# Sixteen groups of attention heads: the first groups' side work dealt out anew, and the loads, clip and norm of two late groups moved

## The chip, the cores and the metric

The kernel runs on one core of a Trainium2 chip. A core has a matrix engine (TensorE, PE in the profile), a vector engine (VectorE, DVE), a scalar engine (ScalarE, ACT), a general engine (GpSimd, POOL) and SyncE (SP), which here only issues transfers. Each engine works through its own list of instructions in order, and waits on semaphores for the others. The metric is the device time of one execution in microseconds; the kernel before takes 945.73 us, the median of three runs (945.61 to 947.5).

## The reference: what is computed

Eight sequences of 512 tokens with 256 channels pass through two layers. Only what matters is shown:

```python
# layer 0
xn = layernorm(x)
x = x + attention(xn) + int8_linear(xn)
# attention: 16 heads of 64, rotary turn of q and k, causal softmax, times v, times Wo, + bo
x_scale = max(|xn|.max() / 127, 1e-5)          # one number for all sequences
x_int8 = clip(round(xn / x_scale), -128, 127)
int8_linear = (x_int8 @ weight_int8.T) * x_scale * weight_scale + bias
# layer 1
xn = layernorm(x)
comparison = (xn @ left) @ (xn @ right).T / 16
x = x + (comparison > threshold) * softmax(comparison + gate_bias) @ xn
      + sigmoid(xr @ W_r) * (relu(xk @ W_k)**2 @ W_v)   # xr, xk mix a token with the one before
```

Since x_scale needs all eight sequences, the int8 part of layer 0 can only begin once all inputs were normed.

## The kernel before, in words

**Groups.** The attention of a sequence is cut into two groups of eight heads. Group `at` (0 to 15) belongs to sequence `at // 2`. Group 0 is written out by hand, groups 1 to 14 are passes of the loop `for at in range(1, last)`, with `last` = 15 (group 14 leaves the loop in the middle), and group 15 with the second layer follows. The text writes (at, run) or (head group, which) where the code does.

**Steps of a group.**
- `project_qk` (L403): q or k of four heads by matmul into pq; ACT moves it to l with the bias (L408); four transfers on SP's queue bring the swapped halves to y (L410).
- `turn_own` multiplies l by a cosine table into h (DVE, L420); `turn_other` multiplies y by a sine table (DVE, L420) and adds it to h (POOL, L435).
- `project_v` (L445): v by matmul in two halves, moved by ACT (L451), written to DRAM; `load_v` reads it back rearranged into vr (L462). vr has one buffer, so the load waits for the matmul `weigh` of the group before.
- A group's scores are done in five runs. `scores(at, run)` is PE (L482). `soften(at, run)` adds the mask and finds the row maximum on DVE (L508), then takes the exponential on ACT with its row sum (L512). `divide(at, run)` takes the reciprocal of the sum on DVE (L523) and multiplies p on POOL (L528). `turn(at, run)` transposes p in 32 x 32 blocks on DVE (L548) into t.
- `weigh(at)` is the matmul of t with vr (av, L565), which needs all five runs turned; `keep_weighed` moves it on ACT (L579); `finish` multiplies by Wo (pw, L365) and adds to x1 (L374).

**Order.** The scheduling is manual: every engine's list follows the order of the calls in the text. In pass `at` of the loop that is scores(at, 0), the last turn of group at - 1, weigh(at - 1), the turns of q and k of later groups, then runs 1 to 4 of group `at` mixed with the projections of groups at + 1 and at + 2.

**Side work.** Input x of a sequence is loaded, its mean and variance taken (`look_at`, statistics L152 to L157: DVE, then one power on POOL), normalised and its largest value found (`prepare`, L170 and L304 on DVE), transposed on PE (`transpose_x`, pxt, L321) and moved by ACT. In the loop, look_at(b + 2) and prepare(b + 2) stand in the second group of a sequence b, from group 1 on, and transpose_x(b + 1) in the first group of sequence b. In group 1 the int8 weights and the constants of layer 1 are spread as well (`spread_rest`, `spread_second`, L285, L140, L141).

**The two groups that complete sequences.** In groups 12 and 13 (`last - 3`, `last - 2`) the int8 part is added to sequences 0 and 1. Their unfinished sums come back from DRAM as x1e (L180) and their normed input as xnl (L183). `quantise` rounds and clips xnl into xq, three instructions on POOL (L190 to L192); `add_quantised` multiplies (acc, L207) and adds. At the end of group 13 the normed first sequence of layer 1 is made (`first_norm`, yn, L170), which PE transposes in the stage after group 14 (pyt, L231). The third sequence's input, xnl_2, is fetched in group 15, and its clip stands on DVE (`clip`, L198, L199), as do those of all later ones.

**Buffers.** Eight PSUM banks go round among all matmul results. The tiles p come from a pool of four buffers, x and vr have one each, and xnl one of its own.

Of the kernel before, what the change touches and what calls it, by code (L numbers as in the profile page):

```python
# [44 lines left out]
def two_layers(  # L45
# [97 lines left out]
    def statistics(src, name, parts=1, power=True):  # L143

        st = small.tile([P, NT, 6], F32, tag="st", name=f"st_{name}", bufs=2)
        mv = small.tile([P, NT, 2], F32, tag="mv", name=f"mv_{name}", bufs=2)
        ve = small.tile([P, NT], F32, tag="ve", name=f"ve_{name}", bufs=2)
        rstd = small.tile([P, NT], F32, tag="rstd", name=f"rstd_{name}", bufs=2)
        for h in range(parts):
            rows = slice(h * NT // parts, (h + 1) * NT // parts)  # L150
            for t in range(NT)[rows]:
                nc.vector.bn_stats(st[:, t, :], src[:, t, :])  # L152
            for t in range(NT)[rows]:
                nc.vector.bn_aggr(mv[:, t, :], st[:, t, :])
            nc.vector.tensor_scalar(ve[:, rows], mv[:, rows, 1], LN_EPS, None, ALU.add)
            if power:
                nc.gpsimd.tensor_tensor(rstd[:, rows], ve[:, rows], mhalf[:, rows], ALU.pow)  # L157
        if power:
            return mv, rstd

        def later():
            nc.gpsimd.tensor_tensor(rstd, ve, mhalf, ALU.pow)
            return mv, rstd

        return later
# [20 lines left out]
    def quantise(b, r, xq):  # L186

        r = r.rearrange("p a n -> p (a n)")
        xq_ = xq.rearrange("p k n -> p (k n)")
        nc.gpsimd.tensor_scalar(r, r, xs[:, 1:2], ROUND, ALU.mult, ALU.add)  # L190
        nc.gpsimd.tensor_scalar(xq_, r, -ROUND, -128.0, ALU.add, ALU.max)
        nc.gpsimd.tensor_scalar(xq_, xq_, 127.0, 127.0, ALU.min, ALU.min)  # L192
# [64 lines left out]
    with ExitStack() as c0:  # L257
# [26 lines left out]
        def spread_rest():  # L284
            nc.vector.tensor_copy(w8b, rest.pop(0).bitcast(I8))  # L285
            nc.gpsimd.tensor_tensor(bob, bob, rw[:, 2, :], ALU.add)
# [143 lines left out]
        def turn_other(at, which):  # L430

            _, y = evicted.pop((at, which))
            h = heads_of[at, which]
            times(y, y, S)
            nc.gpsimd.tensor_tensor(h, h, y, ALU.add)  # L435

        def project_v(at):
            b, g = divmod(at, NH)
            stores[at] = away.tile([4, P, NT * P], F32, tag="v", name=f"va_{at}")
            for half in range(2):  # L440
# [48 lines left out]
        def soften(at, run):  # L489
# [7 lines left out]
            for us in RUNS[run]:  # L497
                if (at, run) == (last, 0):
                    p = qk.tile([P, 2, S], F32, tag="h0", name=f"p_{at}_{us[0]}")
                else:  # L500
                    p = prob.tile([P, 2, S], F32, tag="p", name=f"p_{at}_{us[0]}")
# [16 lines left out]
        def divide(at, run):  # L518
            _, sm, rs = sums_of[at]
            for us in RUNS[run]:  # L520
                first = 2 * PLACE[us[0]]
                which = slice(first, first + 2 * len(us))
                nc.vector.reciprocal(rs[:, which], sm[:, which])  # L523
                for i in us:
                    for e in range(2):
                        c = 2 * PLACE[i] + e
                        p = chances[at, i][:, e, :]
                        nc.gpsimd.tensor_scalar(p, p, rs[:, c : c + 1], 1.0, ALU.mult, ALU.mult)  # L528
# [74 lines left out]
        def round_late(b):  # L603
            r = late[b].rearrange("p a n -> p (a n)")
            nc.gpsimd.tensor_scalar(r, r, xs[:, 1:2], ROUND, ALU.mult, ALU.add)
# [162 lines left out]
        turn_other(1, 0)  # L768
        turn_other(1, 1)
# [16 lines left out]
        divide(0, 1)  # L786
# [3 lines left out]
        scores(0, 2)  # L790
        soften(0, 2)
        project_qk(3, 0)
        transpose_x(1)
        turn_qk(3, 1)
        turn(0, 1)
        divide(0, 2)
        scores(0, 3)
        soften(0, 3)
        project_v(1)
        turn_qk(3, 0)  # L800
        x_next.append(load_x(2))
        turn(0, 2)
        divide(0, 3)
        scores(0, 4)
        soften(0, 4)
        turn(0, 3)
        project(2, 1)
        divide(0, 4)
        for at in range(1, last):
# [20 lines left out]
            load_v(at)  # L830
            divide(at, 0)
# [16 lines left out]
            turn(at, 1)  # L848
            divide(at, 2)
            if g == 1 and b + 2 < B:  # L850
# [3 lines left out]
            if at == 1:  # L854
                spread_rest()
                spread_second()
# [19 lines left out]
            if at == last - 2:  # L876
                first_norm()
# [31 lines left out]
        late[2] = fetch_input(2, work.tile([P, NK, S], F32, tag="xnl", name="xnl_2"))  # L909
# [9 lines left out]
        load_v(at)  # L919
        add_biases(B - 1)  # L920
# [145 lines left out]
```

## Time and profile before

| what | value |
|---|---|
| runs | 945.61, 945.73, 947.5 us |
| profiled execution | 950.06 us |
| its span | 948.3 us |
| PE busy | 927.3 us, 98% of the span |
| DVE, ACT, POOL busy | 784.0, 529.7, 568.3 us |
| mean TensorE clock granted | 0.996 |

The profiled execution is 1.76 us longer than its span, and 4.33 us above the median of the runs. A view called the timeline lists instructions of one engine in order: the start in us from the span's start, the length in us, the engine, the line of the kernel, the operation, out<-in, shapes, how many alike in a row, and in brackets the idle time of the engine before the first, with what ended it. "issue" there means that the profile shows nothing that the engine waited for. The matmuls of fp32 are two records each. A row of windows shows, for a stretch of time, its length, the busy us of PE, of the weight loads (PEld), DVE, ACT and POOL with counts, then the clock granted to TensorE (1.00 is full), the busy share of the DMA engines and the GB/s. Since PE's own busy time includes slow matmuls, idle time and slow stretches are read from the timeline and the windows together.

### The profile page before, as it was taken

What the parts mean: (1) busy time and instruction counts of PE and PEld (TensorE: products, weight loads), DVE (VectorE), ACT (ScalarE), POOL (GpSimd) and SP (SyncE); (2) the same over time, 40 slices, a digit from 0 to 9 for tenths busy, and PEclk for the clock granted to TensorE, in tenths of its full rate; (3) what the DMA queues carried; (4) which work ended last, traced back from release to release, by engine and by line L of the source; (5) the groups of instructions that cost most, each with busy time, mean ns of one, the idle gap of its engine ahead of it and who ended that gap; (6) DMA issues with size and microseconds to landing.
All of it is one profiled execution on the core that took longest, in us unless ns stands there. A gap on an engine that the chain in (4) does not pass through costs nothing.

```text
span 948.3 us, 27434 instructions
## 1 busy us (share of the span) xinstructions
PE 927.3 (98%) x10491; PEld 601.3 (63%) x10491; DVE 784.0 (83%) x2425; ACT 529.7 (56%) x1480; POOL 568.3 (60%) x702
## 2 busy tenths in 40 slices
PE   9999999999999999999999998999999999999998
PEld 5446566656666575657566655666657777777776
DVE  4888988898799789878997896798989588888864
ACT  3565565656564646574656655555567334455553
POOL 3795775655664757557565665989776424444311
PEclk9999999999999999999999999999999999999999
DMA  7666454525443545263444435353344132221110
GB/s 213 187 169 170 113 129 145 123 78 134 150 107 103 127 122 135 70 177 94 110 114 134 114 90 157 113 157 90 91 123 125 46 96 66 67 66 44 32 34 33
DMA packets 60930, 105.40 MB, mean 111 GB/s; under 512 B 7552, under 2 KB 38272, under 8 KB 60800
## 3 DMA queue, kind: packets, MB, share of 16 engines
q1 hardware_dynamic: 58928, 102.01, 39.7%
q10 hardware_dynamic: 1872, 1.64, 0.6%
q8 instruction: 83, 1.36, 0.6%
q14 instruction: 47, 0.39, 0.1%
HBM read 39.14 MB, written 28.84 MB: 72 GB/s over the span
## 4 chain that ended last, share of the span: by engine, by line
PE 94%; DVE 2%; issue 2%; POOL 1%; ACT 1%; DMA 0%; DVEq 0%; POOLq 0%; ACTq 0%
PE pq L403 22%; PE av L565 14%; PE sc L482 13%; PE pw L365 12%; PE pv L445 11%; PE po L725 6%; PE pk L672 3%; PE pg L687 3%; PE pvv L699 3%; PE c L644 2%; PE trc L712 1%; PE plr L242 1%; PE acc L207 1%; PE pyt L231 1%; DVE p L508 1%
## 5 line engine op out<-in xcount | busy, mean ns | idle before, releaser
L512 ACT ACTIVATE p<-p,nm 128x64 f32<-128x64 f32 (+15 forms) x512 | 260.0, 511 | 144.8 <-DVE nm L508 111.1
L528 POOL TENSOR_SCALAR p<-p,rs 128x64 f32<-128x64 f32 (+15 forms) x512 | 269.5, 549 | 44.4 <-DVE rs L523 42.2
L435 POOL TENSOR_TENSOR h<-h,y 128x1024 f32<-128x1024 f32 x64 | 167.0, 2610 | 176.2 <-DVE y L420 97.1
L508 DVE CUSTOM_DVE_ANT_0 p<-sc,cmask 128x64 f32<-128x64 f32 (+15 forms) x512 | 190.4, 434 | 73.8 <-PE sc L482 73.8
L548 DVE STREAM_TRANSPOSE t<-p 128x256 f32<-128x256 f32 (+3 forms) x640 | 192.4, 365 | 20.2 <-POOL p L528 20.2
L482 PE MATMUL sc<-h,h 64*32 64x512 f32 (+15 forms) x4096 | 141.6, 396 | 7.0 <-issue 3.6
L565 PE MATMUL av<-t,vr 32*64 32x384 f32 (+15 forms) x4096 | 130.8, 396 | 6.7 <-issue 6.7
L565 PEld LDWEIGHTS av<-t,vr 32*64 32x64 f32 x4096 | 124.5, 132 | 12.6 <-issue 11.1
L482 PEld LDWEIGHTS sc<-h,h 64*32 64x32 f32 x4096 | 78.6, 106 | 84.1 <-issue 63.2
L408 ACT ACTIVATE l<-pq,cs 128x512 f32<-128x512 f32 x128 | 84.4, 682 | 61.7 <-PE pq L403 52.1
L420 DVE TENSOR_TENSOR y<-y,cs 128x1024 f32<-128x1024 f32 x64 | 111.1, 1736 | 5.1 <-DMA y<-l 4.5
L445 PE MATMUL pv<-wv,xnT 128*128 128x512 f32 x256 | 114.0, 598 | 1.3 <-ACT l L408 1.3
L403 PE MATMUL pq<-xnT,wq 128*128 128x512 f32 x256 | 115.0, 601 | 0.2 <-ACT xnT L324 0.2
L365 PE MATMUL pw<-wo,att 128*128 128x256 f32 x512 | 114.8, 382 | 0.0
L403 PE MATMUL pq<-xnT,wk 128*128 128x512 f32 x256 | 112.9, 593 | 0.0
L365 PEld LDWEIGHTS pw<-wo,att 128*128 128x128 f32 x512 | 95.9, 190 | 18.5 <-issue 6.1
L512 ACT ACTIVATION_READ_ACCUMULATOR p<-p,nm 128x1 f32 x512 | 96.9, 189 | 0.0
L445 PEld LDWEIGHTS pv<-wv,xnT 128*128 128x128 f32 x256 | 47.4, 190 | 59.3 <-issue 54.0
L403 PEld LDWEIGHTS pq<-xnT,wk 128*128 128x128 f32 x256 | 48.6, 190 | 55.6 <-issue 54.9
L420 DVE TENSOR_TENSOR h<-l,cs 128x1024 f32<-128x1024 f32 x64 | 79.7, 1246 | 4.3 <-ACT l L408 4.3
L403 PEld LDWEIGHTS pq<-xnT,wq 128*128 128x128 f32 x256 | 47.4, 191 | 56.4 <-issue 48.8
L579 ACT ACTIVATE att<-av,cs 128x512 f32<-128x512 f32 x64 | 38.8, 689 | 72.4 <-PE av L565 72.4
(113 smaller groups left out, 956.0 us busy)
## 6 DMA issues: line engine op xcount, KB each, us to landing
y<-l SPq DMA_DIRECT2D x256, 128.0 KB, 2.3
va<-v SPq DMA_DIRECT2D x32, 512.0 KB, 3.0
vr<-va SPq DMA_DIRECT2D x64, 256.0 KB, 4.4
x<-in_x SPq DMA_DIRECT2D x15, 512.0 KB, 5.3
xnf<-xnT SPq DMA_DIRECT2D x8, 512.0 KB, 3.3
x1f<-x SPq DMA_DIRECT2D x7, 512.0 KB, 2.6
out<-y SPq DMA_DIRECT2D x14, 256.0 KB, 2.2
cut_wo<-xnf SPq DMA_DIRECT2D x5, 512.0 KB, 4.5
```

The costliest lines, as they stand in the source:

```text
L365: nc.tensor.matmul(pw[:, j, :], atts[at, p][:, tok], wo[:, 4 * (at % NH) + p, :], start=(p == 0), stop=(p == 3),)
L403: nc.tensor.matmul(pb, w[:, g, k, bass.ts(t, P)], xnT[b][:, k, :], start=(k == 0), stop=(k == NK - 1),)
L408: nc.scalar.activation(l[:, t, :], pb, AF.Identity, bias=cs[:, bias : bias + 1])
L420: nc.vector.tensor_tensor(dst, src, table[:, None, :].to_broadcast([P, 2, S]), ALU.mult)
L435: nc.gpsimd.tensor_tensor(h, h, y, ALU.add)
L445: nc.tensor.matmul(pb.rearrange("p (g n) -> p g n", g=2), xnT[b][:, k, bass.ts(2 * half + j, P)], wqkv[2][:, 2 * g : 2 * g + 2, k, :], sta ...
L482: nc.tensor.matmul(scored[at, i][e][j * Q : j * Q + Q, :], q[rows, j % 2, bass.ts(i, Q)], k[rows, j % 2, :n], start=True, stop=True,)
L508: nc.vector.tensor_tensor_reduce(p[:, e, col : col + n], sc, cmask[:, S - n :], -1.0 / L**0.5, BIG, ALU.add, ALU.min, nm[:, c : c + 1],)
L512: nc.scalar.activation(p[:, e, col : col + n], p[:, e, col : col + n], AF.Exp, bias=nm[:, c : c + 1], scale=-1.0, accum_out=sm[:, c : c + 1],)
L528: nc.gpsimd.tensor_scalar(p, p, rs[:, c : c + 1], 1.0, ALU.mult, ALU.mult)
L548: nc.vector.transpose(turned[at][c][:, :, at_ : at_ + (n - 1) * pitch(c) + 1 : pitch(c), :], p[:, :, c * P : c * P + n * Q].rearrange("p e ...
L565: nc.tensor.matmul(banks[j][e * L : e * L + L, i * Q :], vs[at][rows, m, c, bass.ts(e, L)], t[c][rows, e, m * pitch(c) + m : m * pitch(c) ...
```

## The change

In groups 0 and 1:
- the additions of h for q and k of the second four heads of group 0 go from POOL to DVE;
- of runs 1 and 3 of group 0, the division of the last tile (p_12, p_8) goes from POOL to ACT, as Copy with a scale per row;
- q of head group 3 is projected and moved by ACT ahead of the exponentials of run 2; the reciprocals of run 2 stand ahead of the multiplication of y, and the division of run 2 ahead of POOL's addition of h;
- the second half of v of group 1 is projected after the scores of run 4, whose softmax step moves ahead of the turn of run 2, with its p in the buffer of xnl;
- one small DVE instruction (ve) of the second input moves behind the additions.

In groups 1 to 4: look_at(2) and prepare(2) move from group 1 to group 2, the spreads from group 1 to group 4.

In groups 12 and 13: x1e and xnl are fetched after load_v instead of at the start of the pass; the two clipping instructions go from POOL to DVE, behind turn(at, 1); the normalising of `first_norm` moves from the end of group 13 to group 14, behind divide(at, 1). In group 15 xnl_2 is fetched after load_v.

```diff
-            nc.vector.tensor_scalar(ve[:, rows], mv[:, rows, 1], LN_EPS, None, ALU.add)
             if power:
+                nc.vector.tensor_scalar(ve[:, rows], mv[:, rows, 1], LN_EPS, None, ALU.add)
                 nc.gpsimd.tensor_tensor(rstd[:, rows], ve[:, rows], mhalf[:, rows], ALU.pow)
...
         def later():
+            nc.vector.tensor_scalar(ve, mv[:, :, 1], LN_EPS, None, ALU.add)
...
-    def quantise(b, r, xq):
+    def round_input(r):
         r = r.rearrange("p a n -> p (a n)")
-        xq_ = xq.rearrange("p k n -> p (k n)")
         nc.gpsimd.tensor_scalar(r, r, xs[:, 1:2], ROUND, ALU.mult, ALU.add)
-        nc.gpsimd.tensor_scalar(xq_, r, -ROUND, -128.0, ALU.add, ALU.max)
-        nc.gpsimd.tensor_scalar(xq_, xq_, 127.0, 127.0, ALU.min, ALU.min)
...
-            nc.gpsimd.tensor_tensor(h, h, y, ALU.add)
+            (engine or nc.gpsimd).tensor_tensor(h, h, y, ALU.add)
...
+                elif (at, run) == (0, len(RUNS) - 1):
+                    p = work.tile([P, 2, S], F32, tag="xnl", name=f"p_{at}_{us[0]}")
...
-                        nc.gpsimd.tensor_scalar(p, p, rs[:, c : c + 1], 1.0, ALU.mult, ALU.mult)
+                        if on_act and us is RUNS[run][-1]:
+                            nc.scalar.activation(p, p, AF.Copy, scale=rs[:, c : c + 1])
+                        else:
+                            nc.gpsimd.tensor_scalar(p, p, rs[:, c : c + 1], 1.0, ALU.mult, ALU.mult)
...
-        turn_other(1, 0)
-        turn_other(1, 1)
+        turn_other(1, 0, nc.vector)
+        turn_other(1, 1, nc.vector)
...
-        divide(0, 1)
+        divide(0, 1, on_act=True)
         turn_other(2, 0)
         project_qk(3, 1)
         load_v(0)
         scores(0, 2)
+        project_qk(3, 0)
         soften(0, 2)
-        project_qk(3, 0)
         transpose_x(1)
-        turn_qk(3, 1)
+        turn_own(3, 1)
+        divide(0, 2)
+        turn_other(3, 1)
         turn(0, 1)
-        divide(0, 2)
         scores(0, 3)
+        project_v(1, (0,))
         soften(0, 3)
-        project_v(1)
-        turn_qk(3, 0)
-        x_next.append(load_x(2))
-        turn(0, 2)
-        divide(0, 3)
         scores(0, 4)
         soften(0, 4)
+        project_v(1, (1,))
+        turn_qk(3, 0)
+        divide(0, 3, on_act=True)
+        divide(0, 4)
+        turn(0, 2)
+        x_next.append(load_x(2))
         turn(0, 3)
         project(2, 1)
-        divide(0, 4)
...
-            if at in (last - 3, last - 2):
-                s_ = at - last + 3
-                fetch_output(s_, output_tile(f"x1e_{s_}"))
-                xnl = fetch_input(s_, work.tile([P, NK, S], F32, tag="xnl", name=f"xnl_{s_}"))
             scores(at, 0)
...
             load_v(at)
+            if at in (last - 3, last - 2):
+                s_ = at - last + 3
+                fetch_output(s_, output_tile(f"x1e_{s_}"))
+                xnl = fetch_input(s_, work.tile([P, NK, S], F32, tag="xnl", name=f"xnl_{s_}"))
             divide(at, 0)
...
             turn(at, 0)
-            if g == 1 and b + 2 < B:
+            if at == 2:
+                look_at(2)
+            elif at == 4:
+                spread_rest()
+                spread_second()
+            elif g == 1 and 1 <= b < B - 2:
                 look_at(b + 2)
             divide(at, 1)
+            if at == last - 1:
+                first_norm()
             project(at + 1, 0)
             if at in (last - 3, last - 2):
-                xq = work.tile([P, NK, S], BF16, tag="xq", name=f"xq_{s_}")
-                quantise(s_, xnl, xq)
+                round_input(xnl)
...
             turn(at, 1)
+            if at in (last - 3, last - 2):
+                xq = work.tile([P, NK, S], BF16, tag="xq", name=f"xq_{s_}")
+                clip(xnl, xq)
             divide(at, 2)
-            if g == 1 and b + 2 < B:
+            if at == 2:
+                prepare(2)
+            elif g == 1 and 1 <= b < B - 2:
                 prepare(b + 2)
...
             if at == 1:
-                spread_rest()
-                spread_second()
+                nc.gpsimd.tensor_tensor(bob, bob, rw[:, 2, :], ALU.add)
                 add_biases(0)
...
             finish(at - 1)
-            if at == last - 2:
-                first_norm()
...
         fetch(B - 1)
-        late[2] = fetch_input(2, work.tile([P, NK, S], F32, tag="xnl", name="xnl_2"))
...
         load_v(at)
+        late[2] = fetch_input(2, work.tile([P, NK, S], F32, tag="xnl", name="xnl_2"))
```

More of the change, by code (lines that the diff above doesn't have):

```diff
@@ L285, in spread_rest @@
             nc.vector.tensor_copy(w8b, rest.pop(0).bitcast(I8))
-            nc.gpsimd.tensor_tensor(bob, bob, rw[:, 2, :], ALU.add)
         xnT = {}
@@ L428, in turn_own, with turn_other @@
             heads_of[at, which] = h
-        def turn_other(at, which):
+        def turn_other(at, which, engine=None):
             _, y = evicted.pop((at, which))
@@ L434, in turn_other, with project_v @@
             times(y, y, S)
-            nc.gpsimd.tensor_tensor(h, h, y, ALU.add)
-        def project_v(at):
+            (engine or nc.gpsimd).tensor_tensor(h, h, y, ALU.add)
+        def project_v(at, halves=(0, 1)):
             b, g = divmod(at, NH)
-            stores[at] = away.tile([4, P, NT * P], F32, tag="v", name=f"va_{at}")
-            for half in range(2):
+            if 0 in halves:
+                stores[at] = away.tile([4, P, NT * P], F32, tag="v", name=f"va_{at}")
+            for half in halves:
                 v = work.tile([P, 4, 2, P], F32, tag="v", name=f"v_{at}_{half}", bufs=2)
@@ L516, in soften, with divide @@
                     col += n
-        def divide(at, run):
+        def divide(at, run, on_act=False):
             _, sm, rs = sums_of[at]
@@ L603, in round_late @@
         def round_late(b):
-            r = late[b].rearrange("p a n -> p (a n)")
-            nc.gpsimd.tensor_scalar(r, r, xs[:, 1:2], ROUND, ALU.mult, ALU.add)
+            round_input(late[b])
         def clip_late(b):
```

## The prediction

> **What bounds the kernel now.** I read the page first, then the chain that ended last, then TensorE's (PE's) timeline for every idle stretch, then the engine that ended each, and last the clock by windows and the DMA queues. From the page:
>
> ```profile
> span 948.3 us, 27434 instructions
> PE 927.3 (98%) x10491; PEld 601.3 (63%) x10491; DVE 784.0 (83%) x2425; ACT 529.7 (56%) x1480; POOL 568.3 (60%) x702
> PE 94%; DVE 2%; issue 2%; POOL 1%; ACT 1%; DMA 0%; DVEq 0%; POOLq 0%; ACTq 0%
> ```
>
> PE is the bound: 94% of the chain is matmul, and the change leaves the number of matmuls alone. What can move is the 6% (57 us) in which the chain is not on PE, and the slow matmuls behind such waits. An undisturbed group between 131 and 567 us takes 44.3 us, or 45.1 with the transposes of the next x. PE's timeline where groups take longer:
>
> ```profile
> 35.49 3.91 PE L482 MATMUL sc<-h,h 64*32 64x512 f32 x104 [1.50 <-POOL h L435]
> 76.31 9.69 PE L565 MATMUL av<-t,vr 32*64 32x512 f32 x256 [2.29 <-issue]
> 123.70 6.67 PE L565 MATMUL av<-t,vr 32*64 32x512 f32 x197 [1.41 <-issue]
> 149.70 1.04 PE L321 MATMUL pxt<-ident,x 128*128 128x128 f32 x8
> ...
> 584.78 3.16 PE L482 MATMUL sc<-h,h 64*32 64x448 f32 x60 [2.74 <-issue]
> 671.34 8.05 PE L565 MATMUL av<-t,vr 32*64 32x512 f32 x256 [1.67 <-issue]
> 705.68 1.93 PE L482 MATMUL sc<-h,h 64*32 64x512 f32 x40 [1.21 <-POOL h L435]
> 724.45 1.08 PE L482 MATMUL sc<-h,h 64*32 64x352 f32 x27 [0.89 <-issue]
> ```
>
> Columns: start, length, and in brackets the idle time before and its releaser. Where "issue" stands before av, VectorE (DVE) names the cause: its last two transposes of the group before end at that moment, held by GpSimd (POOL):
>
> ```profile
> 75.76 0.77 DVE L548 STREAM_TRANSPOSE t<-p 128x256 f32<-128x256 f32 x2 [1.06 <-POOL p L528]
> 123.16 0.77 DVE L548 STREAM_TRANSPOSE t<-p 128x256 f32<-128x256 f32 x2 [1.06 <-POOL p L528]
> 149.77 0.20 DVE L523 RECIPROCAL rs<-sm 128x4 f32<-128x4 f32 x2
> 670.80 0.77 DVE L548 STREAM_TRANSPOSE t<-p 128x256 f32<-128x256 f32 x2 [1.06 <-POOL p L528]
> ```
>
> The wait at 582 is another kind: DVE and POOL are not late. SP's queue issued 1 MB just before, and the DMA view shows no instruction packet (q8) from 576.5 to 582 us while q1 moved 1.56 MB, then one in 582 to 584:
>
> ```profile
> 576.58 0.51 SPq L180 DMA_DIRECT2D x1e<-x1f  x1
> 577.13 0.43 SPq L183 DMA_DIRECT2D xnl<-xnf  x1
> 581.32 2.67 SPq L462 DMA_DIRECT2D vr<-va  x4
> 582.00:584.00 2.00, 0.04 (x2) 0.00 (x0) 0.00 (x0) 1.58 (x3) 2.00 (x4) 1.00 0.92 246
> 586.00:588.00 2.00, 2.00 (x44) 0.90 (x29) 1.51 (x9) 1.02 (x3) 2.00 (x1) 0.50 0.41 82
> ```
>
> In the two windows (busy of PE, PEld, DVE, ACT, POOL; clock; DMA) PE stands still, then runs at clock 0.50. I read it as PE out of instructions, its fetch queued behind x1e and xnl.
>
> **The change part by part.** Names of groups are values of `at`.
>
> (a) Groups 0 and 1, to the first av. The two adds of h leave POOL (2.35 us each, from 29.58 to 35.44 with the wait between them) for DVE. DVE adds of two SBUF operands are not in the trace; the nearest row is DVE's L420, 1.22 us when POOL is still. So y_1_0 29.5, add 30.7, y_1_1 31.9, add 33.1: PE arrives at 32.93, its 1.50 us go, and the first softmax step starts near 34.2 instead of 36.60. POOL loses four divisions of p_12 and four of p_8; ACT gains them. ACT's Copy from SBUF with a scale per row is not in that stage; bounds are ACT's exponentials of these widths without their accumulator read (0.63, 0.36, 0.50, 0.44 us), so 1.9 us for each four, and half of that. The small edits here cost nothing: ve's 0.17 us on DVE falls before DVE's first softmax step and lets POOL start on x_1 at 33.3 instead of 35.4; run 4's p in xnl's buffer frees its softmax step from turn(0,2); the later half of pv is the same PE work behind 0.6 us of scores.
> The new wait: ACT's first division needs the reciprocal that DVE makes after turn(0,0), near 47.3, while ACT is done with its exponentials near 45.3. Behind it on ACT are l_3_1, l_3_0 (pulled ahead: 4 x 0.62) and the next exponentials (4.05): 47.3 + 1.9 + 2.4 + 4.05 = 55.7. DVE's reciprocal for run 2 now stands ahead of y_3_1 and waits for them, with 1.5 to 3 us idle. Then y_3_1 1.2, turn 2.8, softmax steps 2.8 and 0.7, h and y of (3,0) 2.4, reciprocals 0.3, turn 2.8: 68.7. POOL's last adds and divisions (2.36, then 1.9 and 0.93 from about 65.7) end at 70.9, turn 3 and 4 near 72.5. av can start near 72.8 against 76.31: gain 3.5, between 0 (the ACT wait eats it) and 5.5 (all four idle stretches of PE to there, 1.50 + 0.49 + 1.25 + 2.29). PE gets there near 70, so some 2.5 us idle stay.
>
> That wait's half clock stays too: 78 to 80 us ran at 0.50 after 2.29 us of idle, and that av took 9.69 us where others take 8.05, while 1.41 and 1.67 us of idle were followed by clock 1.00. [...]
>
> (b) Group 1 sheds look_at(2), prepare(2) and the spreads: 1.37 + 0.37 + 0.17 + 1.95 + 1.22 + 0.42 + 0.22 + 0.29 = 6.0 us of DVE. It is there that DVE falls behind (no idle time on DVE from 104.6 to 122.1 us). Its last turn comes over 3 us earlier, the wait of 1.41 goes: gain 1.4 (0 to 1.4). The spreads in group 4 are 0.9 us in DVE's idle time before its run 2 there: nothing; if it were gone, 0.9. POOL's one power (1.02 us) moves from group 1 to 2: nothing, POOL waits for DVE there.
>
> (c) Group 2 gets them. look_at (1.9 us) falls into DVE's idle 3.0 us before run 2: nothing. prepare does not: DVE finishes the reciprocals of run 2 at 149.97, as PE comes to the transposes of x_2 (149.70). Normalising takes 1.95 (the same four at 195.08 in group 3), PE's last five transposes 0.65 more: 152.6 instead of 150.74. Cost 1.8, from 0 (if DVE gains on PE) to 3.4 (idle long enough for a half clock, 1.6). ACT's copies of xnT shift along; behind them amax 1.22 delays no PE, which has run 3 in hand.
>
> (d) Group 12: x1e and xnl are issued after vr instead of before it, past one step of SP's queue, at about 584 in before's time. The fetch at 582 then finds only x1_6. Gain: run 1 of the scores took 6.77 us where others take 2.05, the next pq 7.50 instead of 7.06: 5.1. Between 0 (it stands anyway) and 5.1. [...] xnl lands near 590, POOL wants it at 595.9 or, without the wait, 591.
>
> (e) Groups 12 and 13: POOL drops 3.65 + 4.33 and 3.65 + 3.64; DVE takes two clips, 0.69 to 1.0 and 0.43 to 1.15 (rows L198, L199 of the second layer), and in group 13 sheds the norm (1.97). POOL ran without a gap from 640.5 to 669.3 and DVE waited for it at 658.24 (0.97), 660.02 (0.35) and 670.80. All that goes, and with it the 1.67 before av: gain 1.7 (0 to 1.7). The norm lands in DVE's idle 3.04 us before 689.62 of group 14: nothing; if that cover were gone, up to 1.97. yn is wanted at 711.
>
> (f) xnl_2 goes behind vr of group 15: the 0.89 at 724 has x_7 and xnl_2 in flight before it. I take 0.5 (0 to 0.9). The 1.21 at 705 is POOL's chain of group 14, untouched.
>
> Sum: 3.5 + 1.4 - 1.8 + 5.1 + 1.7 + 0.5 = 10.4, so the profiled execution would go from 950.06 (span 948.3 and 1.76 around it) to 939.7. But that execution is 4.33 above the median of 945.73; whether the timed runs pay (d) is not known. I count half of it there, 2.5: 945.73 - 5.3 - 2.5 = 937.9, forecast 938.0.
>
> **The rivals.**
> - The stall of (d) belongs to the profiled execution alone. For it: 4.33 of excess against a 5.1 us stall. Against it: the runs themselves differ by 1.9. Then 945.73 - 5.3 = 940.4.
> - ACT becomes the bound of group 0, as its divisions hold up the evictions: (a) gives 0, the rest 4.3: 941.4. For it: DVE's new wait; against it: POOL loses 8 us there.
> - Slower: the starvation only moves. After the change vr (1 MB) and the loads go out in one burst in groups 12, 13 and 15, across the fetch seen after 586. Price 5.1 for each place, 15.3 for three: 945.73 - 5.3 - 2.5 + 15.3 = 953.2. One such place still leaves 943.0; from two on (948.1) it decides. Against it: PE uses up instructions slowly in the pq that follows.
> - It does not do what it says: (a) gives 0, the wait of (c) grows to 3.4 and (d) is 0: 1.4 - 3.4 + 1.7 + 0.5 = 0.2, so 945.5.
>
> **How the numbers follow.** Forecast 0.48 (its own range 934 to 942), stall only profiled 0.16, ACT bound 0.12, burst 0.13, no effect 0.11. A change under 0.2% (1.9 us) can't be told from none. Faster 0.48 + 0.16 + 0.12 = 0.76, same 0.11, slower 0.13. The range runs from 933.5 (forecast, all of (d) in the timed runs and the half clock gone: 945.73 - 10.4 - 1.6 = 933.7) to 947.5, which leaves out the burst.
>
> **What would show it.** (a) av starts near 72.8, ACT divides from about 47.3, DVE idles before L523 near 54. (b) no idle before the second av. (c) 1 to 2.5 us idle before the pxt of group 2. (d) q8 packets between 576 and 582, no stall in run 1 of group 12. (e) no idle before av at 671. Wrong if PE starves behind the new bursts, or if POOL slows DVE's adds and clips.

## The result

| | kernel before | changed kernel |
|---|---|---|
| median, us | 946.62 (945.61 to 947.64) | 939.62 (938.92 to 941.44) |
| profiled execution, us | 950.06 | 939.1 |
| its span, us | 948.3 | 937.2 |
| ratio | | 0.9913, 95% interval 0.9886 to 0.994 |

The changed kernel is 7.0 us (0.7%) faster by the medians, 8.2 us by the ratio (5.7 to 10.8 by its interval). From the page of the changed kernel:

```profile
span 937.2 us, 27414 instructions
PE 923.8 (99%) x10491; PEld 600.8 (64%) x10491; DVE 787.4 (84%) x2431; ACT 533.0 (57%) x1488; POOL 540.0 (58%) x688
PE 92%; DVE 4%; issue 1%; ACT 1%; POOL 1%; SPq 0%; DMA 0%; DVEq 0%; ACTq 0%; POOLq 0%
```

POOL gives up 28 us, DVE and ACT take 3.4 and 3.3; PE is the bound as before. PE's timeline of the changed kernel at the places that the prediction named:

```profile
72.57 8.05 PE L568 MATMUL av<-t,vr 32*64 32x512 f32 x256 [2.31 <-issue]
...
118.84 6.10 PE L568 MATMUL av<-t,vr 32*64 32x512 f32 x175 [0.86 <-issue]
125.37 2.24 PE L568 MATMUL av<-t,vr 32*64 32x192 f32 x81 [0.43 <-issue]
127.54 2.56 PE L480 MATMUL sc<-h,h 64*32 64x448 f32 x64
...
139.03 7.13 PE L443 MATMUL pv<-wv,xnT 128*128 128x512 f32 x16
146.68 0.30 PE L318 MATMUL pxt<-ident,x 128*128 128x128 f32 x1 [0.51 <-PE pv L443]
147.23 0.33 PE L318 MATMUL pxt<-ident,x 128*128 128x128 f32 x1 [0.25 <-DVE x L171]
147.82 1.14 PE L318 MATMUL pxt<-ident,x 128*128 128x128 f32 x6 [0.26 <-DVE x L171]
148.89 2.39 PE L480 MATMUL sc<-h,h 64*32 64x320 f32 x80
...
578.37 2.43 PE L480 MATMUL sc<-h,h 64*32 64x448 f32 x64
...
661.65 8.02 PE L568 MATMUL av<-t,vr 32*64 32x512 f32 x256
```

The first av starts at 72.57 instead of 76.31 and takes 8.05 us instead of 9.69. The second still waits, 0.86 us. New are the three waits ahead of pxt, for DVE's normalising of x_2. Run 1 of group 12 passes without a stall, and the av of group 13 without a wait.

Cutting the two profiled executions at the starts of av shows where the time went. The starts: 76.31, 123.70, 168.84, 573.30, 624.21, 671.34, 714.11, 744.04 before; 72.57, 118.84, 167.07, 570.57, 616.63, 661.65, 704.38, 732.70 after.

| stretch | before | after | gain | term |
|---|---|---|---|---|
| start to first av | 76.31 | 72.57 | +3.74 | (a) 3.5 |
| first av to second | 47.39 | 46.27 | +1.12 | (b) 1.4 |
| second to third (group 2) | 45.14 | 48.23 | -3.09 | (c) -1.8 |
| third av to that of group 11 | 404.46 | 403.50 | +0.96 | none |
| group 11 to 12 | 50.91 | 46.06 | +4.85 | (d) 5.1 |
| group 12 to 13 | 47.13 | 45.02 | +2.11 | (e) 1.7 |
| group 13 to 14 | 42.77 | 42.73 | +0.04 | none |
| group 14 to 15 | 29.93 | 28.32 | +1.61 | (f) 0.5 |
| last av to the end | 204.26 | 204.50 | -0.24 | none |

They add up to 11.1, the difference of the spans. Some agree by luck: the +1.12 is 1.64 of a half clock that did not come, 0.55 of a shorter wait, and 1.07 lost at run 1 of group 1 (3.12 us to the next pq instead of 2.05). Which terms belong to the kernel and which to one execution is what the experiments settle.

### The profile page after: what moved, and what is told of

Its sections match the earlier page's. It is cut to its first block, busy times and chain, and to the rows that moved or that the text cites. A ratio compares the mean times of both kernels' runs of the same rounds, so it can differ in the third digit from the quotient of the medians.

```text
span 937.2 us, 27414 instructions
## 1 busy us (share of the span) xinstructions
PE 923.8 (99%) x10491; PEld 600.8 (64%) x10491; DVE 787.4 (84%) x2431; ACT 533.0 (57%) x1488; POOL 540.0 (58%) x688
## 3 DMA queue, kind: packets, MB, share of 16 engines
q10 hardware_dynamic: 1872, 1.64, 0.7%
## 4 chain that ended last, share of the span: by engine, by line
PE 92%; DVE 4%; issue 1%; ACT 1%; POOL 1%; SPq 0%; DMA 0%; DVEq 0%; ACTq 0%; POOLq 0%
PE pq L400 22%; PE av L568 14%; PE sc L480 13%; PE pw L362 12%; PE pv L443 10%; PE po L727 5%; PE pg L689 3%; PE pvv L701 3%; PE pk L674 3%; PE trc L714 1%; PE plr L240 1%; PE c L646 1%; DVE t L551 1%; PE acc L205 1%; DVE p L508 1%
## 5 line engine op out<-in xcount | busy, mean ns | idle before, releaser
L531 POOL TENSOR_SCALAR p<-p,rs 128x512 f32<-128x512 f32 (+4 forms) x504 | 263.3, 543 | 44.0 <-DVE rs L523 41.9
L432 POOL TENSOR_TENSOR h<-h,y 128x1024 f32<-128x1024 f32 x62 | 161.0, 2596 | 188.9 <-DVE y L417 106.6
L480 PE MATMUL sc<-h,h 64*32 64x416 f32 (+15 forms) x4096 | 138.7, 393 | 1.9 <-POOL h L432 1.2
L568 PE MATMUL av<-t,vr 32*64 32x192 f32 (+15 forms) x4096 | 128.8, 392 | 4.0 <-issue 4.0
L405 ACT ACTIVATE l<-pq,cs 128x512 f32<-128x512 f32 x128 | 84.7, 683 | 66.8 <-PE pq L400 54.4
L443 PEld LDWEIGHTS pv<-wv,xnT 128*128 128x128 f32 x256 | 47.3, 190 | 57.9 <-issue 54.1
L400 PEld LDWEIGHTS pq<-xnT,wq 128*128 128x128 f32 x256 | 47.2, 190 | 56.0 <-issue 48.8
```

The costliest lines, as they stand in the source:

```text
L400: nc.tensor.matmul(pb, w[:, g, k, bass.ts(t, P)], xnT[b][:, k, :], start=(k == 0), stop=(k == NK - 1),)
L405: nc.scalar.activation(l[:, t, :], pb, AF.Identity, bias=cs[:, bias : bias + 1])
L432: (engine or nc.gpsimd).tensor_tensor(h, h, y, ALU.add)
L443: nc.tensor.matmul(pb.rearrange("p (g n) -> p g n", g=2), xnT[b][:, k, bass.ts(2 * half + j, P)], wqkv[2][:, 2 * g : 2 * g + 2, k, :], sta ...
L480: nc.tensor.matmul(scored[at, i][e][j * Q : j * Q + Q, :], q[rows, j % 2, bass.ts(i, Q)], k[rows, j % 2, :n], start=True, stop=True,)
L568: nc.tensor.matmul(banks[j][e * L : e * L + L, i * Q :], vs[at][rows, m, c, bass.ts(e, L)], t[c][rows, e, m * pitch(c) + m : m * pitch(c) ...
```

## The experiments

Each ran beside the kernel before on the same chip, which was 948.22, 947.6 and 948.31 us in the three sets of four. Since the changed kernel's ratio has an interval of 0.3% to either side, a difference of under some 3 us between two variants is read from the stretches of the traces, and the medians are given beside it.

### The kernel before again

No edit.

> The kernel before, unchanged, to see whether the stall of 2.74 us at 584.8 us and the half clock behind the 2.29 us wait at 76 us belong to the kernel or to the one execution shown. Theory 1 (the stall belongs to the kernel): the new profiled execution shows an idle PE of 2 to 3 us ahead of the second part of run 1 of group 12, and the interval between the starts of av of groups 11 and 12 (573.3 and 624.2 in the profile shown) is again near 50.9 us. Theory 2 (it is that one execution): the interval is near 46.1 us, as in the changed kernel (570.6 to 616.6), and the profiled execution is 3 to 5 us shorter than the 950.06 us shown. The same question for the first av: 9.69 us again (the clock falls by a rule on idle time) or 8.05 (by chance). Time against the kernel before: 0.

Measured: 947.18 us, ratio 0.9995 (0.9978 to 1.0011); profiled 948.07. PE's timeline, and the windows:

```profile
581.04 0.94 PE L482 MATMUL sc<-h,h 64*32 64x448 f32 x4
584.00 2.69 PE L482 MATMUL sc<-h,h 64*32 64x448 f32 x60 [2.01 <-issue]
```

```profile
582.00:584.00 2.00, 0.00 (x0) 0.00 (x1) 0.46 (x1) 1.52 (x3) 2.00 (x3) 1.00 0.68 154
...
586.00:588.00 2.00, 2.00 (x20) 1.15 (x9) 1.94 (x13) 2.00 (x9) 1.81 (x1) 0.50 0.58 115
```

The stall is there again, at the same four matmuls into run 1, with the half clock behind it, and the stretch from av of group 11 to 12 takes 50.38 us: theory 1. The first av waited 2.17 us and took 9.69 us, as in the execution shown, with clocks of 0.69, 0.50 and 0.96 in the windows of 2 us from 76 to 82 us.

### (d) alone

```diff
-            if at in (last - 3, last - 2):
-                s_ = at - last + 3
-                fetch_output(s_, output_tile(f"x1e_{s_}"))
-                xnl = fetch_input(s_, work.tile([P, NK, S], F32, tag="xnl", name=f"xnl_{s_}"))
             scores(at, 0)
...
             load_v(at)
+            if at in (last - 3, last - 2):
+                s_ = at - last + 3
+                fetch_output(s_, output_tile(f"x1e_{s_}"))
+                xnl = fetch_input(s_, work.tile([P, NK, S], F32, tag="xnl", name=f"xnl_{s_}"))
```

> The kernel before with one part of the change alone, (d): x1e and xnl of groups 12 and 13 are issued behind the four loads of vr. If the stall is PE's instruction fetch behind these two loads and is paid in every execution: the interval from av of group 11 to av of group 12 goes from 50.9 to about 46 us, and the time falls by 5.1 us. If it is paid in half of them, as forecast: 2.5 us. If it belongs to the profiled execution alone: 0, within 1 us. If the burst starves PE at another place: 5 us slower for each.

Measured: 945.29 us against 948.22, ratio 0.9973 (0.9956 to 0.999): 2.6 us, 0.9 to 4.2. PE's timeline:

```profile
580.16 2.57 PE L482 MATMUL sc<-h,h 64*32 64x448 f32 x64
582.67 7.13 PE L403 MATMUL pq<-xnT,wq 128*128 128x512 f32 x16
...
648.07 1.05 PE L207 MATMUL acc<-w8b,xq 128*128 128x256 bf16 x8 [1.05 <-ACT p L512]
...
666.64 8.06 PE L565 MATMUL av<-t,vr 32*64 32x512 f32 x256 [1.86 <-issue]
```

The stall is gone, the stretch takes 46.27 us instead of 50.38 to 50.91. Part of it is given back one group on: POOL's first clip takes 4.54 us there instead of 3.65, its second ends at 648.02, acc waits 1.05 us for it, and the stretch to the av of group 13 takes 48.07 us instead of 47.13 and 47.38. What is left of the difference between 4.1 to 4.6 in the stretch and 2.6 in the time lies within the interval of the ratio.

### (d) undone

The reverse of that diff, in the changed kernel.

> The changed kernel with (d) undone: x1e and xnl of groups 12 and 13 are issued at the start of the pass again, all else as changed. If the order of the loads makes the stall, it is back in run 1 of group 12: 5.1 us slower than the changed kernel if every execution pays it (944.7 against 939.6), 2.5 us by the forecast's half. If the stall was a matter of phase that the earlier groups' gains shifted away, or of one execution: 0, and the interval between the av of groups 11 and 12 stays near 46.1 us.

Measured: 943.45 us, ratio 0.9946 (0.9927 to 0.9965), against 0.9913 and 0.9917 of the changed kernel: about 3 us slower.

```profile
577.43 0.96 PE L480 MATMUL sc<-h,h 64*32 64x448 f32 x8
581.11 3.55 PE L480 MATMUL sc<-h,h 64*32 64x448 f32 x56 [2.73 <-issue]
```

The stretch is back at 50.86 us; in group 13 the same run stalls 1.27 us. So the order of the loads makes the stall: it is in all three profiled executions with x1e and xnl ahead of vr, and over 0.3 us in none of the eleven with them behind. The executions shown of before and of the changed kernel have 83 instruction packets of 16 KB each on queue q8; that they are PE's is inferred from what follows them. In before one starts at 582.08 and PE goes on at 584.78, 2.70 us later. At short stalls that are left in the changed kernel, packets start at 79.30, 122.88, 396.36 and 485.02, and PE goes on at 81.70, 125.37, 398.84 and 487.35, 2.33 to 2.49 us later. What it is about the loads that goes with the late packet, their bytes or their number, no run separates.

### The changed kernel again

No edit.

> The changed kernel, unchanged, as the yardstick of the three beside it, and for two questions. If the half clock behind the first av is chance and not a rule on idle time: about half of the executions have a mean clock of 1.000, the others 0.998 or less, and those of the lower clock are about 1.7 us longer for each 0.002, as in the kernel before, where 14 executions at 0.996 take 949.1 us, 13 at 0.998 take 946.8 and 5 at 1.000 take 945.2 on the mean. If it is a rule: all executions have the same clock. And the time: 939.6 again, which is 0.9% under the kernel before (948.2 there, so 939.6 to 940 here).

Measured: 940.06 us, ratio 0.9917 (0.9887 to 0.9947). One execution has a mean clock of 0.996 (942.15 us), four 0.998 (939.9 on the mean), one 1.000 (937.73): the half clock differs from one execution to the next, so the length of the idle time alone does not decide it. The same stretch of the first av, in the changed kernel's first and in this execution:

```profile
74.00:76.00 2.00, 2.00 (x79) 2.00 (x69) 2.00 (x9) 2.00 (x7) 0.00 (x0) 1.00 0.62 141
```

```profile
74.00:76.00 2.00, 2.00 (x30) 1.88 (x22) 2.00 (x11) 2.00 (x7) 0.00 (x0) 0.50 0.78 176
```

PE had waited 2.31 and 2.32 us; one ran at full clock, the other at half, and its av took 9.54 us. In the windows of 2 us from 14 to 930 us, ten of the 14 profiled executions show half clock, 14 stretches of it, of 3.40 to 3.44 us each. What sets apart the executions with the same wait, these runs do not show.

### (a): ACT's divisions back on POOL

```diff
-        divide(0, 1, on_act=True)
+        divide(0, 1)
...
-        divide(0, 3, on_act=True)
+        divide(0, 3)
```

> The changed kernel with the divisions of p_12 and p_8 of group 0 back on POOL (eight of 0.4 to 0.6 us), the rest of (a) kept. If ACT's help is what brings the first av forward: POOL is late by 1.9 + 1.9 us, the first av starts 2 to 3.5 us later (74.5 to 76 instead of 72.6 us) and the kernel is 2 to 3.5 us slower than the changed one. If it is only the additions of h on DVE that bring it: av at 72.6 still, 0 us. If ACT's new wait for the reciprocal had cost something, the kernel is faster.

Measured: 939.8 us, ratio 0.992 (0.9891 to 0.9949); the changed kernel beside it 940.06. The 2 to 3.5 us that were expected if ACT's help brings the av forward did not come.

### (a): the additions of h back on POOL

```diff
-        turn_other(1, 0, nc.vector)
-        turn_other(1, 1, nc.vector)
+        turn_other(1, 0)
+        turn_other(1, 1)
```

> The changed kernel with the two additions of h of head group 1 back on POOL (2.35 us each), the rest of (a) kept. If they bring the first av forward: PE waits 1.0 to 1.5 us again for POOL's h before the first scores (35.5 us in the kernel before), the input's normalising on POOL is 2.4 us later, and the first av comes at 74 to 75 us instead of 72.6: 1.5 to 2 us slower. If the chain of DVE behind them has slack: the wait at the first scores comes back but av starts at 72.6 still, with a shorter wait: 0 us.

Measured: 941.43 us, ratio 0.9927 (0.99 to 0.9953): 1.4 us slower by the medians.

### (a): the new order alone

Both of these diffs together.

> The changed kernel with the additions of h and the eight divisions both back on POOL: of (a) only the new order in groups 0 and 1 is kept. Counted from PE's first pq, the first av starts at 67.0 to 67.6 us in the kernel before and at 63.6 to 64.0 in the changed one; with the divisions back it was 64.7, with the additions back 65.3. If the two sum (0.8 + 1.5) and the new order gives the rest: 66.1, and the kernel is 2 to 2.5 us slower than the changed one. If the order is worth nothing, as the forecast had it: 67.3, 3.5 us slower.

Measured: 942.94 us, ratio 0.9947 (0.9928 to 0.9966): about 2.9 us slower. PE's timeline of the three, first without ACT's divisions, then without DVE's additions, then without both:

```profile
73.11 2.89 PE L568 MATMUL av<-t,vr 32*64 32x512 f32 x20 [3.11 <-issue]
```

```profile
34.79 3.91 PE L480 MATMUL sc<-h,h 64*32 64x512 f32 x104 [1.02 <-POOL h L432]
...
73.78 2.21 PE L568 MATMUL av<-t,vr 32*64 32x512 f32 x18 [2.32 <-issue]
```

```profile
75.35 1.20 PE L568 MATMUL av<-t,vr 32*64 32x512 f32 x12 [3.10 <-issue]
```

Counted from PE's first pq, since executions differ by up to 0.6 us before it, the first av starts at 67.0 to 67.6 us with the old front and at 63.5 to 64.0 with the new one (seven of eight executions; 64.7 in one where PE had waited 1.49 us for DVE's softmax step at 61.9). Without ACT's divisions it is 64.7, without DVE's additions 65.3, without both 66.8. So the additions are worth 1.5 us, ACT's help 0.8, both 2.9, and the order 0.6. Each comes from one execution: the 0.8 and the 0.6 are no larger than the scatter between executions with the same front (63.5 to 64.7, 67.0 to 67.6), the 1.5 and the 2.9 are larger. ACT's 0.8 did not show in the time: the changed kernel and the one without it differ by 0.3 us the other way.

### (c): the normalising of x_2 earlier

```diff
             project(at + 1, 0)
+            if at == 2:
+                prepare(2)
...
             divide(at, 2)
-            if at == 2:
-                prepare(2)
-            elif g == 1 and 1 <= b < B - 2:
+            if g == 1 and 1 <= b < B - 2:
                 prepare(b + 2)
```

> The changed kernel with prepare(2) ahead of the scores and softmax step of run 2 of group 2, where DVE is idle for 2.07 us, instead of behind divide(2, 2). If term (c) is DVE's normalising standing just ahead of PE's transposes (from the start of pv to the first scores of run 3 took 9.86 us against 7.94 before), the three idle stretches of PE ahead of pxt (0.51, 0.25 and 0.26 us) go and the kernel is 1.9 us faster than the changed one: 937.7. Rival: DVE is only moved, so that the softmax step of run 2 comes 1 to 2 us later (the normalising takes 1.95 and the greatest value 1.22, the idle time there is 2.07) and the last turn of group 2 or POOL's divisions hold up av by as much: 0, or up to 1 us slower.

Measured: 938.62 us, ratio 0.9904 (0.9884 to 0.9923): 1.0 to 1.4 us under the changed kernel. DVE, then PE:

```profile
137.75 2.03 DVE L171 TENSOR_SCALAR x<-x,mv_a,rstd_a 128x256 f32<-128x256 f32 x4 [1.01 <-POOL rstd_a L157]
139.81 1.22 DVE L301 TENSOR_REDUCE amax<-x 128x1 f32<-128x1024 f32 x1
```

```profile
119.74 8.28 PE L568 MATMUL av<-t,vr 32*64 32x512 f32 x256 [1.41 <-issue]
...
146.14 1.04 PE L318 MATMUL pxt<-ident,x 128*128 128x128 f32 x8
```

The waits ahead of pxt are gone, and the stretch takes 45.54 us instead of 47.2 to 48.9. The softmax step of run 2 starts 2.7 us later than it did (140.95 against 138.28) and nobody waits for it: the rival falls. The second av still waits.

### (b), (c): the input back in group 1

```diff
-            if at == 2:
-                look_at(2)
-            elif at == 4:
+            if at == 4:
                 spread_rest()
                 spread_second()
-            elif g == 1 and 1 <= b < B - 2:
+            elif g == 1 and b < B - 2:
                 look_at(b + 2)
...
-            if at == 2:
-                prepare(2)
-            elif g == 1 and 1 <= b < B - 2:
+            if g == 1 and b < B - 2:
                 prepare(b + 2)
```

> The changed kernel with look_at(2) and prepare(2) back in group 1 (5.1 us of DVE), the spreads left in group 4. By the forecast's terms, group 2 gets its wait ahead of the transposes back (c: 1.8, measured 1.9 us in that stretch) and group 1 keeps its wait of 1.4 at the second av instead of 0.4 to 1.5 now: 0.9 to 2 us faster than the changed kernel, 938 to 939. If the DVE work makes group 1 late by more than it saves in group 2: the second av waits over 2.5 us and the kernel is slower than the changed one.

Measured: 937.81 us, ratio 0.9897 (0.9863 to 0.9932): about 2 us under the changed kernel.

```profile
119.26 8.05 PE L568 MATMUL av<-t,vr 32*64 32x512 f32 x256 [1.31 <-issue]
...
145.26 1.04 PE L318 MATMUL pxt<-ident,x 128*128 128x128 f32 x8
```

With 5.1 us of DVE work back in group 1 the second av waits 1.31 us, against 0.86 and 1.53 in the changed kernel and 1.41 with the earlier normalising, which have none of it there (0.1 to 1.5 over the eight executions with the change's groups 1 and 2). So DVE's load is not the main thing that holds the second av, and moving it cost group 2 more than it gave group 1.

### The earlier normalising, and POOL's bias rows later

The diff of the earlier normalising, and:

```diff
-            if at == 1:
-                nc.gpsimd.tensor_tensor(bob, bob, rw[:, 2, :], ALU.add)
-                add_biases(0)
             project_v(at + 1)
...
             divide(at, 4)
+            if at == 1:
+                nc.gpsimd.tensor_tensor(bob, bob, rw[:, 2, :], ALU.add)
+                add_biases(0)
```

> The changed kernel with two edits: prepare(2) ahead of the scores of run 2 of group 2, and in group 1 POOL's addition of the bias rows and add_biases(0) (0.72 + 2.79 us) behind divide(1, 4) instead of ahead of POOL's addition of h and the division of run 3. In the changed kernel DVE waits for that division from 111.2 to 113.9 us (2.63), its reciprocal of run 4 stands behind it, and the second av waits 0.86 us. If POOL's side work is what holds the second av: that wait goes, 0.9 us, and with the 1.6 us of the earlier normalising (47.18 to 45.54 in that interval) the kernel is 2.5 us under the changed one: 937.1. Rival: the last division still comes 1.06 us behind the reciprocal of run 4, which hangs on ACT's exponentials of run 4, so that the wait stays at 0.5 to 1.4: 938 to 938.6, no faster than with the earlier normalising alone.

Measured: 935.74 us, ratio 0.9878 (0.9847 to 0.9909); the changed kernel beside it 940.06. In the changed kernel, POOL and DVE ahead of the second av:

```profile
107.73 2.79 POOL L352 TENSOR_TENSOR x<-x,rw 128x256 f32<-128x256 f32 x4
110.47 2.35 POOL L432 TENSOR_TENSOR h<-h,y 128x1024 f32<-128x1024 f32 x1
112.80 3.65 POOL L531 TENSOR_SCALAR p<-p,rs 128x320 f32<-128x320 f32 x8
```

```profile
113.87 1.48 DVE L551 STREAM_TRANSPOSE t<-p 128x256 f32<-128x256 f32 x5 [2.63 <-POOL p L531]
...
118.29 0.77 DVE L551 STREAM_TRANSPOSE t<-p 128x256 f32<-128x256 f32 x2 [1.06 <-POOL p L531]
```

and with the bias rows later, DVE and PE:

```profile
110.89 2.83 DVE L551 STREAM_TRANSPOSE t<-p 128x256 f32<-128x256 f32 x10
113.66 0.12 DVE L523 RECIPROCAL rs<-sm 128x2 f32<-128x2 f32 x1
114.84 0.77 DVE L551 STREAM_TRANSPOSE t<-p 128x256 f32<-128x256 f32 x2 [1.06 <-POOL p L531]
```

```profile
115.85 1.95 PE L480 MATMUL sc<-h,h 64*32 64x512 f32 x48
117.74 8.02 PE L568 MATMUL av<-t,vr 32*64 32x512 f32 x256
```

DVE's 2.63 us wait for POOL is gone, its last transposes end at 115.6 instead of 119.1, and the second av starts without a wait. What held it was POOL's queue: 3.5 us of bias rows ahead of the addition of h and the division that DVE turns next. The rival falls, since the 1.06 us of the last division now lies under PE's scores. The gain by the medians is 4.3 us where 2.5 were expected; the two stretches take 45.20 and 45.13 us instead of 46.27 to 47.36 and 47.86 to 48.23 in the changed kernel's two profiled executions, so 1.1 to 2.2 and 2.7 to 3.1; the 47.36 has a half clock in it (9.54 us for av), the 45.20 has none.

### (e): the clips back on POOL

```diff
-                round_input(xnl)
+                xq = work.tile([P, NK, S], BF16, tag="xq", name=f"xq_{s_}")
+                quantise(s_, xnl, xq)
...
             turn(at, 1)
-            if at in (last - 3, last - 2):
-                xq = work.tile([P, NK, S], BF16, tag="xq", name=f"xq_{s_}")
-                clip(xnl, xq)
```

> The changed kernel with the two clipping instructions of groups 12 and 13 back on POOL, behind the rounding, and the norm left in group 14. If POOL's gapless stretch is what held up the av of group 13, as term (e) says: the interval from av of group 12 to av of group 13 goes from 45.0 to about 47.1 us with a wait of 1.7 us ahead of av, and the kernel is 1.7 to 2.1 us slower than the changed one (941.8 to 942). If the norm on DVE was the cause: 45.0 still, 0 us.

Measured: 942.14 us, ratio 0.994 (0.9921 to 0.9959), about 2.1 us slower. POOL, then PE:

```profile
638.17 4.56 POOL L192 TENSOR_SCALAR xq<-xnl 128x1024 bf16<-128x1024 f32 x1
642.82 3.64 POOL L193 TENSOR_SCALAR xq<-xq 128x1024 bf16<-128x1024 bf16 x1
```

```profile
646.51 1.05 PE L213 MATMUL acc<-w8b,xq 128*128 128x256 bf16 x8 [1.05 <-ACT p L520]
...
664.39 8.05 PE L576 MATMUL av<-t,vr 32*64 32x512 f32 x256 [1.18 <-PE sc L488]
```

acc reads what POOL's second clip writes, and starts as it ends at 646.46 (the exponential that the view names is no input of acc); av waits for POOL's last division, which ends at 663.8. The stretch takes 47.41 us instead of 45.02.

### (e): the norm back in group 13

```diff
-            if at == last - 1:
-                first_norm()
             project(at + 1, 0)
...
             finish(at - 1)
+            if at == last - 2:
+                first_norm()
```

> The changed kernel with the normalising of first_norm back at the end of group 13 (1.97 us on DVE ahead of turn(13, 3)), the clips left on DVE. If POOL was the late one: the av of group 13 starts in time, the interval stays at 45.0 us and the time is that of the changed kernel. If DVE, with the clips and the norm, is late there: av waits 1 to 2 us, and the kernel is as much slower.

Measured: 941.02 us, ratio 0.9939 (0.9914 to 0.9964), 1 to 2 us slower. DVE and PE:

```profile
655.43 3.92 DVE L171 TENSOR_SCALAR yn<-x1e,mv_b,rstd_b 128x256 f32<-128x256 f32 x4
659.28 2.83 DVE L551 STREAM_TRANSPOSE t<-p 128x256 f32<-128x256 f32 x10
```

```profile
663.77 8.06 PE L568 MATMUL av<-t,vr 32*64 32x512 f32 x256 [1.87 <-issue]
```

The wait at av is back, 1.87 us, with POOL idle for 4.02 us at that moment: this time DVE is late. The theory that POOL was the late one falls as the whole cause. The norm takes 3.92 us here instead of 1.97, most of it beside POOL's addition of x1e (655.74 to 658.24): one of its four instructions fills the window from 656 to 658 us by itself, where each takes 0.54 to 0.59 us in the kernel before.

## Why the prediction was right, and where not

The forecast was 938.0, from 945.73 less 7.7. Measured were 939.62 and, later, 940.06. Over the executions beside the experiments the kernel before takes 948.0 us (median of 78), so the base of three runs was 2.3 us low, and the change gained about 8. The time, 1.6 to 2.1 us above the forecast, lies within its range and its case's own. It does not tell the forecast from the first rival, whose 940.4 is nearer; the traces do, for the stall of (d) is there in each of the three profiled executions with the old order of the loads.

**The base and the clock.** Much of the runs' spread goes with the half clock. The 78 executions group by mean clock: on the mean 945.4 us at 1.000, 946.9 at 0.998, 948.9 at 0.996, 950.4 at 0.994. But the ten at 1.000 alone span 943.5 to 948.0. In the executions shown a half-clock stretch adds 1.64 and 1.49 us to an av (9.69 and 9.54 us instead of 8.05); the kernel before most often has one or two (0.998 and 0.996 are 53 of the 78), the changed one none or one in nine executions of ten. The step that the half clock stays at the first av, since it followed 2.29 us of idle time, took one execution for a rule. After 2.17 to 2.32 us it came in eight of twelve profiled executions; after 3.10 us it did not come (the new order alone), after 3.11 it did (ACT's divisions back). It came after 1.90 us at the second av (the loads alone), and after 1.19 us of waits ahead of the transposes of x_2 (POOL's clips back). So the length of the wait alone, from 1.19 to 3.11 us, does not decide it, and what does is open. What should have stood there, for before and after alike, is a chance of 1.6 us: eight of twelve, as found.

**(a)** Sum right: 3.5 forecast, 3.74 in the pair, 3.5 counted from the first pq. The working holds in detail: ACT divides from 47.24 (near 47.3), its four divisions take 1.71 us (1.9), the addition on DVE 1.22 us (1.22), the last transposes end at 72.79 (near 72.5), av starts at 72.57 (near 72.8), 2.31 us of idle time stay (some 2.5). DVE's idle time ahead of y_3_1 was 0.5 + 0.6, less than the 1.5 to 3 expected. That the small edits cost and give nothing is neither shown nor refuted: the order alone gives 0.6 us in one execution, no more than the scatter. And ACT, which the rival feared to hold things up, did not, and its help does not show in the time.

**(b)** "Its last turn comes over 3 us earlier, the wait of 1.41 goes" failed. DVE was freed and then waited 2.63 us for POOL, whose bias rows stood ahead of the division. The wait at the second av went from 1.41, 1.60 and 1.90 us in three executions with the old order of group 1 to 0.1 to 1.5, 0.7 on the mean, in the eight that keep (b) and (c) as the change has them: 0.9 gained, and the rest only when the bias rows went. The question that was skipped is what is late next, once DVE is not: it was POOL, busy without a break from 101.29 to 116.45. Why the wait differs so much among those eight is open.

**(c)** Mechanism and size right where it was placed: from pv to run 3 it takes 9.86 us instead of 7.94, so 1.9 for 1.8 forecast. The rest of the 3.09, 1.16 us, was lost in av and run 1 (0.72 + 0.44); in av PE stands idle for 0.43 us and goes on at 125.37, 2.49 us after an instruction packet starts. Stretches of 47.2 to 48.9 us in the eight executions with (c) as changed show a cost of 2 to 3.7. In one, without the clips on DVE, a half clock followed that idle time (147.4 to 150.8 us), and its stretch of 48.9 us is near the bound of 3.4 that the prediction named.

**(d)** Right: the stall goes, 5.1 forecast for the profiled execution and 4.85 found; over the executions 50.4 to 50.9 us become 46.1 to 46.9, 4.3 on the mean. The sign came too: instruction packets start at 576.38 and 580.65 in the changed kernel, where before had none between 574.55 and 582.08. The rivals that it belongs to one execution, and that it moves into the bursts of groups 12, 13 and 15, fall: of the kernels with the change's order none stalled over 0.3 us there. The half that was counted in the timed runs is close to what they showed (2.6 alone, about 3 when undone), but by luck: the stall is paid in every execution that was profiled, and alone a part is given back in group 13. The half clock behind it is not paid in every run, since ten of the 78 have a mean clock of 1.000; whether all of them pay the idle time is not shown. In the three profiled executions with the old order the stall was 2.01, 2.73 and 2.74 us of idle time, with a half clock behind it.

**(e)** 1.7 forecast, 2.11 found, and the cause half right. "All that goes, and with it the 1.67" named POOL as what was late and gave the norm's leaving no price of its own. A row of the kernel before spoke against it, POOL's last division there:

```profile
669.83 0.93 POOL L528 TENSOR_SCALAR p<-p,rs 128x256 f32<-128x256 f32 x2 [0.52 <-DVE rs L523]
```

POOL, gapless until 669.3, waited here for DVE's reciprocal, which stood behind the norm and the turn. Either half, put back alone, brings back 1.9 to 2.4 us of the stretch: POOL's clips or DVE's norm each make the chain to the last turn late by itself.

**(f)** 0.5 forecast and 1.61 found, but the kernel before repeated has the stretch at 28.32 us too, as the changed one. Over the executions it is 29.3 before (three) and 28.7 after (eleven). A gain of 0.6 is less than what executions of one kernel differ by there.

With the means of the executions instead of one pair, the terms are 3.5 + 0.9 - 2.6 + 4.3 + 2.2 + 0.6 = 8.9, near the 8 measured. The sum of 10.4 was over by what (b), (c) and (d) missed.

## What to carry to other kernels

When a change frees one engine, ask which engine the freed one waits for next, and look at the whole queue ahead of that instruction: here 3.5 us of bias rows on POOL, movable at no cost that the times show, were the wait that moving 6 us of DVE work did not remove. Where two engines are each late for the same wait, undoing one shows nothing of the other, so both must go, and an undo of each must be tried before one is called the cause. And compare stretches over several executions before a microsecond is believed: a half clock that comes in one execution and not in the next puts one pair of profiles 1.6 us off at a single place.

## What the runs showed of the chip

- PE's half clock comes in stretches of 3.40 to 3.44 us: 14 of them between 14 and 930 us, in ten of the 14 profiled executions. After a wait of 2.17 to 2.32 us ahead of the first av it came in eight of twelve executions; of the two with a longer wait, 3.10 and 3.11 us, it came in the second alone. It also came once after 1.90 us and once after 1.19 us, and why is open. In the executions shown it adds 1.49 to 1.64 us to an av.
- PE goes on 2.33 to 2.70 us after an instruction packet of 16 KB starts, at the five stalls shown. With 1 MB of loads (x1e and xnl) issued ahead of vr, PE stood idle for 2.01 to 2.74 us in run 1 of group 12, in three profiled executions; with them behind vr, for no more than 0.3 us, in eleven.
- The normalising of four 128x256 tiles on DVE takes 1.97 us beside POOL's divisions, in the kernel before, and 3.92 us with the norm back in group 13, where POOL's addition of x1e and u (655.74 to 658.24) runs beside it. One of its four instructions takes at least 2 us there; in the kernel before each takes 0.54 to 0.59. Why it is longer there, no run shows.
